# A four-layer graph network on one core: layer 3's last product in four quadrants, the last LSTM units first and alone, two small tasks later

## The chip, the cores and the metric

The kernel runs on one core of a Trainium2 chip. A core has TensorE (PE, matrix products into PSUM), VectorE (DVE), ScalarE (ACT, table functions and copies), GpSimd (POOL) and SyncE (SP, which here issues the loads and stores). Each works through its own queue of instructions in order; they meet at semaphores. The metric is the device time of one execution in microseconds.

## The reference, cut to what matters

The input x has 128 graphs of 64 nodes with 256 features, in fp32. Four layers follow each other, each as `x = layernorm(x + layer(x))`. Layer 0 is a graph convolution with two batch normalisations, layer 1 a Chebyshev step with attention and a feed-forward net, layer 2 two graph convolutions followed by LSTMs, layer 3 graph attention. The change touches layers 2 and 3:

```python
# layer 2, after two graph convolutions
for p in range(1, MAX_SKIP + 1):                     # 1, 2, 3, 4
    nw = Tv // p
    wins = h[:, :nw * p, :].reshape(Bv * nw, p, Hd)
    last = _lstm_last(Wih[p - 1], Whh[p - 1], bih[p - 1], bhh[p - 1], wins)
    idx = jnp.arange(nw) * p + (p - 1)
    h = h.at[:, idx, :].set(last.reshape(Bv, nw, Hd))
# layer 3
Wh = jnp.einsum('bnf,fo->bno', h, W)
s1 = Wh @ a1
s2 = Wh @ a2
e = s1[:, :, None] + s2[:, None, :]
e = jnp.where(e >= 0, e, ALPHA * e)
e = jnp.where(adj_matrix[None] == 0, -jnp.inf, e)
attention = jax.nn.softmax(e, axis=-1)
h_prime = jnp.einsum('bij,bjo->bio', attention, Wh)
```

An LSTM with window p walks through p nodes one after the other, and the LSTM with window p + 1 reads what the one before wrote. So for one group of graphs the four windows are a chain, and inside a window the p steps are a chain too.

## The kernel before, in words

**Tiling.** The 128 graphs are 16 blocks of 8 graphs. A block is 4 tiles of two graphs: 128 partitions (2 graphs of 64 nodes) by 256 features. Four blocks make a group of 32 graphs; layer 2's LSTMs work on groups, with features on the partitions (tile h). There are four PSUM buffers of 128x1024 (PS, named ps in the profile) and a stock of temporaries of the same size (mem, named t, and later also freed parts of x, h, wL, wA and rows).

**The plan.** Nothing is ordered by hand. Each piece of work is a Python generator (first_block, end_block, block, gcn_block, unit, last_block) that yields steps `step(engine, us, ...)`, and `flow` at build time picks, again and again, which generator goes on. It keeps a clock for each engine, and for each running generator a time at which its next step's inputs are there. The key is the line

```python
soon = max(t + margin.get(e, 0.0), free[e])
```

where t is that time, `free[e]` the time at which the engine is free, and the margin 2.0 us on TensorE and 0.5 on VectorE and ScalarE. The smallest key is emitted next; ties go to the stream with the lower priority number. So a step whose inputs are there only just now is put behind one whose inputs have been there for longer than the margin. The order made in this way is fixed in the program; on the chip each engine follows it, whatever the true durations are.

**Streams.** A stream has a width (how many of its generators run at a time) and a priority. There are two calls of `flow`: one for layer 0 up to its second normalisation, and one for all the rest. In the second, in order of priority: lending of buffers (0), `extra` (1 task each for layer 2's bias rows, gcn_rows, and layer 3's score columns, score_columns; priority 0), weight loads (1), `end` (the 8 half-blocks of layer 3 for the last group, width 4, priority 2), `gcn` (3), `seq` (layer 0's end and layer 1, width 6, priority 4), the LSTM units (5) and `last` (the 12 whole blocks of layer 3 for groups 0 to 2, width 4, priority 6).

**LSTM units.** A unit is an LSTM with window p over some windows of one group: unit(p, g, w0, nw, b0, nb). Window 1 is done in gcn_block (products at L950). Window 4 is one unit for each of groups 0 to 2, and two halves of 16 graphs, 256 columns, for group 3. Whole units use seven products in place of eight for a step (stage1 to stage4, products at L1022; gates at L1060 to L1102). The halves use plain_steps: products of the input at L1159 and of the hidden state at L1161, gates at L1164. The first step of any unit is L950 with gates at L962. The last three units of the list are (4, 2) and the two halves of (4, 3). Before the change they stand in two streams of priority 5, width 2 each: `units[:-2]` and `units[-2:]`.

**A block of layer 3.** last_block(i, t0, nt) handles nt tiles, four for a whole block and two for a half-block. It gathers h on ScalarE (L1362), transposes (L338), adds x (L1373), normalises (bn_stats L270, a power on GpSimd L306, L309 and ScalarE L312), transposes again (L332), copies to xT on ScalarE (L1384), multiplies with W and the score columns (L1397; copies L1407 and L1409), builds e (GpSimd L1417, PE L1421 and L1422, VectorE L1426 to L1430), takes exp with row sums on ScalarE (L1434), reciprocals of the sums on VectorE (L1436), transposes e in 64x64 pieces (L1442), copies them (L1444), multiplies them with Wh (L1450), scales by the reciprocal sums and adds x on VectorE (L1455), normalises and stores (L1461). The product L1450 has for each tile two 64x64 products, one for each graph, from upper partitions to upper ones and from lower to lower.

Of the kernel before, what the change touches and what calls it, by code (L numbers as in the profile page):

```python
# [11 lines left out]
ALU = mybir.AluOpType  # L12
# [3 lines left out]
P = 128  # L16
B, N, D = 128, 64, 256
# [16 lines left out]
def kernel(ctx: ExitStack, tc: tile.TileContext, a: dict, out: bass.AP):  # L34
    nc = tc.nc
    V, S, G, T = nc.vector, nc.scalar, nc.gpsimd, nc.tensor
# [5 lines left out]
    def bc_last(ap, n):  # L42

        return ap.unsqueeze(2).to_broadcast([ap.shape[0], ap.shape[1], n])

    def tm(s):

        return s.rearrange("p (t d) -> p t d", t=NT)

    def fm(s):  # L50

        return s.rearrange("p (c k) -> p c k", c=2)
# [9 lines left out]
    class Stock:  # L62


        def __init__(self, items):
            self.items, self.free, self.shut = [], [], {}
            self.add(items, 0.0)
# [30 lines left out]
    class Stream:  # L98
# [3 lines left out]

        def __init__(self, width, prio, tasks):
            self.width, self.prio, self.tasks, self.n = width, prio, tasks, 0

    done = {}

# [3 lines left out]
    def ready(*keys):  # L113

        if all(k in done for k in keys):
            return max([0.0] + [done[k] for k in keys])
        return None

    def step(e, us, ps=0, sl=0, waits=True, at=None, tbl=None):

        return (e, us, ps, sl, waits, at, tbl)

    def flow(streams, margin):
# [6 lines left out]
        free = dict.fromkeys("TVSGQ", 0.0)  # L135
        table, running, now, seq = None, [], 0.0, 0
        while True:
            for s in streams:
                while s.tasks and s.n < s.width:
                    cond, body, peak = s.tasks[0]  # L140
                    t = 0.0 if cond is None else cond()
# [27 lines left out]
            for r in running:  # L169
                e, us, ps, sl, _, at, tbl = r[2]  # L170
                at = at() if callable(at) else at
                if r[2][5] is not None and at is None:
                    continue
                t = r[3] if at is None else at
                soon = max(t + margin.get(e, 0.0), free[e])
                t = max(t, free[e])
                if (ps <= 0 or len(PS.free) >= ps) and (sl <= 0 or (len(mem.free) >= sl and safe(r, sl))):
                    if ps > 0:
                        t = max(t, PS.free[0][0])
                        soon = max(soon, PS.free[0][0])  # L180
                    if sl > 0:
                        t = max(t, heapq.nsmallest(sl, mem.free)[-1][0])
                        soon = max(soon, t)
                    if best is None or soon < least - 1e-9:
                        best, when, least = r, t, soon
            assert best is not None, "no task can go on"
            e, us, ps, sl, waits, at, tbl = best[2]
# [22 lines left out]
    def ctile(shape, name, pool=cp):  # L210
        return pool.tile(shape, F32, tag=name, name=name)
# [12 lines left out]
    PS = Stock([ctile([P, NT * D], f"ps{j}", psp) for j in range(4)])  # L224
# [16 lines left out]
    halves = slice(0, N), slice(N, P)  # L241
    for s in range(2):
        h = halves[s]
# [141 lines left out]
    with c0:  # L385
# [195 lines left out]
        tasks = [(None, lambda i=i: first_block(i), 2) for i in blocks]  # L581
# [769 lines left out]
    def last_block(i, t0=0, nt=NT):  # L1351
# [3 lines left out]
        x = tm(mem[s_x])[:, :nt, :]  # L1355
        nc.sync.dma_start(x, XD[i][:, t0 : t0 + nt, :])
        r = nt / NT
# [9 lines left out]
        ps = PS.take()  # L1367
        px = tm(PS[ps])[:, :nt, :]
# [9 lines left out]
        ps = PS.take()  # L1378
        s_xT = mem.take()
        px = fm(PS[ps])[:, :, : nt * P]  # L1380
        to_fm(px, x)
        yield step("S", 0.1 + r, ps=-1)
        xT = fm(mem[s_xT])[:, :, : nt * P]
        S.copy(xT, px)  # L1384
        PS.give(ps)
        s12 = sm.tile([P, NT, 2], F32, tag="s12", name="s12")
        for t in range(0, nt, 2):
            end = t == nt - 2
            yield step("T", 1.75, ps=1, sl=int(t == 0))
            ps = PS.take()  # L1390
            pw = fm(PS[ps])
            if t == 0:
                s_w = mem.take()
                Wh = tm(mem[s_w])
            for j in range(2):
                for k in range(2):
# [4 lines left out]
                        start=(k == 0),  # L1401
                        stop=(k == 1),
# [13 lines left out]
        e, aT, d = (mem[s_e][:, j * nt * N : (j + 1) * nt * N].rearrange("p (t m) -> p t m", t=nt) for j in range(3))  # L1416
        G.tensor_tensor(d, bc_mid(unit2, nt), bc_last(s12[:, :nt, 1], N), ALU.mult)  # L1417
        yield step("T", 0.1 + 0.9 * r, ps=1)
        ps = PS.take()
# [12 lines left out]
        sums = sm.tile([P, NT], F32, tag="sums3", name="sums3")  # L1432
        for t in range(nt):
            S.activation(e[:, t, :], e[:, t, :], AF.Exp, bias=mx[:, t : t + 1], accum_out=sums[:, t : t + 1])  # L1434
        yield step("V", 0.2, waits=False)
        V.reciprocal(sums[:, :nt], sums[:, :nt])  # L1436
        yield step("T", 0.1 + 0.5 * r, ps=1)
        ps = PS.take()
        pt = PS[ps][:, : nt * N].rearrange("p (t m) -> p t m", t=nt)
# [3 lines left out]
        yield step("S", 0.15 + 0.3 * r, ps=-1)  # L1443
        S.copy(aT, pt)  # L1444
        PS.give(ps)
        yield step("T", 0.1 + 1.8 * r, ps=1)
        ps = PS.take()
        for t in range(nt):
            for h in halves:
                T.matmul(tm(PS[ps])[h, t, :], aT[h, t, :], Wh[h, t, :], start=True, stop=True)  # L1450
        mem.give(s_e)
        mem.give(s_w)
        yield step("V", 1.7 * r, ps=-1)
        for t in range(nt):
            V.scalar_tensor_tensor(  # L1455
                x[:, t, :], tm(PS[ps])[:, t, :], sums[:, t : t + 1], x[:, t, :], ALU.mult, ALU.add
            )
        PS.give(ps)
        yield from ln_steps_act(x)
        yield step("Q", 3.0)  # L1460
# [8 lines left out]
    for i in blocks:  # L1469
        while n < at_end.get(i, NBLK):  # L1470
            j = ends[n]
# [27 lines left out]
    for g in range(NG - 1):  # L1499
        read = [("read", i) for i in range(4 * g, 4 * g + 4)]  # L1500
        again = lambda g=g: mem.add(Hs[4 * g : 4 * g + 4], Clock.end)
        lends.append(Stream(1, 0, [(lambda read=read: ready(*read), again, 0)]))
    extra = [(None, gcn_rows, 1), (None, score_columns, 1)]
    gcn = [
        (
            lambda i=i: ready(("rows",), ("l1", i), *[("h", j) for j in range(4 * (i // 4), 4 * (i // 4) + 4)])
# [34 lines left out]
    units = []  # L1541
# [12 lines left out]
    def last_of(i, *part):  # L1554
# [10 lines left out]
            Stream(4, 2, end),  # L1565
            Stream(2, 3, gcn),
            Stream(6, 4, seq),
            Stream(2, 5, units[:-2]),
            Stream(2, 5, units[-2:]),
            Stream(4, 6, last),  # L1570
        ],
        MARGIN,
# [49 lines left out]
```

## Time and profile before

| | |
|---|---|
| median of 3 runs | 2446.64 us (2445.72 to 2447.99) |
| the profiled execution | 2449.05 us; its span, first to last instruction, 2447.3 us |
| TensorE busy | 2362.6 us, 97% of the span |
| VectorE, ScalarE, GpSimd busy | 1208.8, 1152.1, 565.7 us |
| mean granted TensorE clock | 0.984 |
| L1450, the product that changes | 256 records; 12 blocks of 16, 8 half-blocks of 8 |
| L1384, the copy to xT | 0.99 us for 128x1024, 0.57 us for 128x512 |
| L1455, scaling and adding | 64 instructions of 0.476 us |
| ACT table loads at L1434 | 8, of 1.28 us each |

A profile line of the order of time has the start in us from the first instruction, the length, the engine, the line of the kernel, the operation, the tile written and the tiles read, the shapes and how many instructions were merged; in brackets the idle time of the engine before it and what ended that. PEld is TensorE's loading of weights. An fp32 product stands as two records of MATMUL.

### The profile page before, as it was taken

How to read it: one execution, taken by the hardware profiler on the slowest of the kernel's cores; microseconds unless marked ns; L12 is line 12 of the kernel's file. 1: busy time of each engine (PE TensorE's matmuls, PEld its weight loads, DVE VectorE, ACT ScalarE, POOL GpSimd, SP SyncE). 2: the span in 40 equal slices, each digit the busy share in tenths (PEclk: the TensorE clock that was granted, in tenths of full speed). 3: DMA queues.
4: the chain of work that ended last, by engine and by line, in shares of the span. 5: the costliest groups of instructions: out<-in, count | busy, mean ns of one | idle time of the engine just before them, and what ended most of it. 6: DMA issues, size and time to landing. Idle time of an engine off the chain costs nothing.

```text
span 2447.3 us, 33911 instructions
## 1 busy us (share of the span) xinstructions
PE 2362.6 (97%) x13700; PEld 1807.8 (74%) x13700; DVE 1208.8 (49%) x2868; ACT 1152.1 (47%) x2086; POOL 565.7 (23%) x426
## 2 busy tenths in 40 slices
PE   8999889989999999999999999999999999999986
PEld 5544566766775767666667888999999888888864
DVE  4542378564665455464442433354444554543465
ACT  2255454533444544444444444444435555653574
POOL 0000034231422233232322222222222222221111
PEclk9999899999999999999999999999999999999998
DMA  5110111100000000000010000000001001000201
GB/s 171 45 59 0 31 36 35 35 9 10 1 18 7 12 1 18 10 27 9 27 50 2 18 1 1 14 5 1 1 1 35 1 18 35 18 9 18 65 31 52
DMA packets 40973, 57.47 MB, mean 23 GB/s; under 512 B 4592, under 2 KB 33904, under 8 KB 40816
## 3 DMA queue, kind: packets, MB, share of 16 engines
q1 hardware_dynamic: 39712, 54.22, 6.8%
q8 instruction: 107, 1.75, 0.3%
q10 hardware_dynamic: 1104, 1.08, 0.1%
q14 instruction: 50, 0.41, 0.1%
HBM read 38.52 MB, written 16.78 MB: 23 GB/s over the span
## 4 chain that ended last, share of the span: by engine, by line
PE 73%; DVE 6%; ACT 4%; POOL 2%; issue 1%; POOLq 0%; ACTq 0%; DVEq 0%
PE ps L1022 24%; PE ps L950 13%; PE ps L344 10%; PE ps L356 5%; PE ps L833 4%; PE ps L320 3%; PE ps L703 2%; PE ps L1397 2%; PE ps L1159 2%; PE ps L1161 2%; DVE ln_st L270 1%; PE ps L332 1%; PE ps L776 1%; PE ps L1450 1%; ACT x L312 1%
## 5 line engine op out<-in xcount | busy, mean ns | idle before, releaser
L1022 PE MATMUL ps<-x,x 128*128 128x256 f32 x832 | 203.2, 379 | 0.7 <-DVE x L1090 0.7
L1022 PEld LDWEIGHTS ps<-x,x 128*128 128x128 f32 x832 | 155.0, 190 | 19.9 <-issue 1.1
L312 ACT ACTIVATE x<-x,ln_nm,ln_rs 128x256 f32<-128x256 f32 x176 | 92.9, 592 | 112.8 <-DVE ln_nm L309 112.8
L1022 PE MATMUL ps<-t,x 128*128 128x256 f32 x576 | 137.7, 380 | 0.0
L1022 PEld LDWEIGHTS ps<-t,x 128*128 128x128 f32 x576 | 108.4, 190 | 14.5 <-issue 0.4
L344 PE MATMUL ps<-t,W1T 128*128 128x512 f32 x256 | 115.1, 593 | 0.0
L306 POOL TENSOR_TENSOR ln_rs<-ln_rs,neghalf 128x4 f32<-128x4 f32 (+1 forms) x72 | 69.4, 964 | 189.7 <-DVE ln_rs L272 167.9
L950 PE MATMUL ps<-t,wL 128*128 128x512 f32 x216 | 94.5, 594 | 1.8 <-ACT t L1248 1.8
L292 POOL TENSOR_TENSOR ln_rs<-ln_rs,neghalf 128x4 f32<-128x4 f32 x32 | 35.9, 1122 | 239.5 <-DVE ln_rs L272 239.0
L950 PE MATMUL ps<-h,x 128*128 128x256 f32 x384 | 86.8, 379 | 0.0
L270 DVE BATCH_NORM_STATS2 ln_st<-x 128x6 f32<-128x256 f32 x224 | 85.5, 403 | 0.4
L962 ACT ACTIVATE t<-ps,bih 128x512 f32<-128x512 f32 (+3 forms) x108 | 63.5, 640 | 44.5 <-PE ps L950 44.4
L344 PE MATMUL ps<-t,wA 128*128 128x512 f32 x176 | 81.5, 608 | 2.6 <-ACT t L679 2.6
L1022 PE MATMUL ps<-h,x 128*128 128x256 f32 x320 | 82.5, 380 | 0.0
L1081 DVE COPY t<-ps 128x256 f32<-128x256 f32 (+2 forms) x58 | 21.6, 373 | 120.5 <-PE ps L1022 120.2
L344 PEld LDWEIGHTS ps<-t,W1T 128*128 128x128 f32 x256 | 46.3, 190 | 46.4 <-issue 46.4
L950 PEld LDWEIGHTS ps<-h,x 128*128 128x128 f32 x384 | 72.8, 190 | 10.2 <-issue 0.5
L950 PE MATMUL ps<-h,wL 128*128 128x192 f32 (+2 forms) x432 | 79.8, 338 | 0.0
L950 PEld LDWEIGHTS ps<-t,wL 128*128 128x128 f32 x216 | 40.7, 190 | 50.8 <-issue 47.1
L1098 ACT ACTIVATE x<-x,bih 128x512 f32<-128x512 f32 (+2 forms) x65 | 42.2, 650 | 76.2 <-DVE x L1088 73.9
L962 ACT ACTIVATE x<-ps,bih 128x512 f32<-128x512 f32 (+3 forms) x94 | 54.8, 636 | 45.6 <-PE ps L950 45.6
L950 PEld LDWEIGHTS ps<-h,wL 128*128 128x128 f32 x432 | 65.6, 190 | 11.4 <-issue 10.5
(681 smaller groups left out, 5765.3 us busy)
## 6 DMA issues: line engine op xcount, KB each, us to landing
t<-in_x_dram SPq DMA_DIRECT2D x28, 512.0 KB, 4.0
xd<-x SPq DMA_DIRECT2D x16, 512.0 KB, 2.6
x<-xd SPq DMA_DIRECT2D x5, 512.0 KB, 3.3
out_dram<-x SPq DMA_DIRECT2D x5, 512.0 KB, 2.9
wL<-in_L_gnn_Wih_dram SPq DMA_DIRECT2D x2, 1024.0 KB, 5.1
x<-in_L_gnn_Whh_dram SPq DMA_DIRECT2D x2, 1024.0 KB, 4.8
h<-in_x_dram SPq DMA_DIRECT2D x3, 512.0 KB, 5.0
t<-xd SPq DMA_DIRECT2D x3, 512.0 KB, 3.7
```

The lines of the kernel that those rows point to most:

```text
L270: V.bn_stats(st[:, t, :], y[:, t, :])
L306: G.tensor_tensor(rs, rs, neghalf[:, :n], ALU.pow)
L312: S.activation(y[:, t, :], y[:, t, :], AF.Identity, scale=rs[:, t : t + 1], bias=nm[:, t : t + 1])
L320: T.matmul(ps[:, c, t * P : (t + 1) * P], y[:, t, c * P : (c + 1) * P], mT, start=True, stop=True,)
L344: T.matmul(ps[:, c, :], w[:, k, (off + c) * P : (off + c + 1) * P], yT[:, k, :], start=(k == 0), stop=(k == nk - 1),)
L356: T.matmul(ps[:, t, :], yT[:, k, t * P : (t + 1) * P], w[:, k, :], start=(k == 0), stop=(k == nk - 1),)
L703: T.matmul(pv[r * N : (r + 1) * N, b, :, :], x1T[:, k, b * N : (b + 1) * N], Wv_par[:, k, r, :, :], start=(k == 0), stop=(k == 1),)
L833: T.matmul(tm(PS[ps])[:, t, :], fm(mem[gs[k // 2]])[:, k % 2, t * P : (t + 1) * P], W2[:, k, :], start=(k == 0), stop=(k == 3),)
L950: T.matmul(spread(fm(PS[ps])[:, j, :n], q), WL[p][0][:, k, m], x_of(0, q)[:, k], start=(k == 0), stop=(k == 1),)
L962: S.activation(of(sl)[:, j], fm(PS[ps])[:, j, :n], AF.Tanh if g == 2 else AF.Sigmoid, bias=bias(g, c))
L1022: T.matmul(dst, WS[p][name](k, g), y[:, k], start=first and k == 0, stop=k == 1, skip_group_check=not first)
L1159: T.matmul(shaped(dst), WL[p][0][:, k, m], x[:, k], start=(k == 0), stop=False)
```

## The change

Four edits are made together.

1. **The product L1450 in four quadrants.** For odd tiles, the two graphs change places in xT: the copy into xT becomes three copies, one of the even tiles and two of the odd tiles' halves. With that, Wh, the scores and e of odd tiles have their graphs swapped. The product of an odd tile then goes from upper partitions to lower ones and from lower to upper, which puts the graphs back, and the four products of two tiles use the four quadrants of the array, odd tiles in another PSUM bank than even ones.
2. **The softmax's scaling earlier.** e is multiplied by the reciprocal sums before its transpose, so that what follows the product is two additions and not four scaled ones. The step now counts as one that the next must wait for.
3. **The last three units.** They get a stream of their own, of width 1 (one at a time), priority 1.5, and marked urgent: for their steps `flow` leaves out the margin on every engine.
4. **The small tasks.** gcn_rows may begin only when layer 1's block 3 has begun, score_columns only after that and when layer 1's block 0 is done.

```diff
-        def __init__(self, width, prio, tasks):
+        def __init__(self, width, prio, tasks, urgent=False):
             self.width, self.prio, self.tasks, self.n = width, prio, tasks, 0
+            self.urgent = urgent
...
-                soon = max(t + margin.get(e, 0.0), free[e])
+                soon = max(t if r[6].urgent else t + margin.get(e, 0.0), free[e])
...
-        yield step("S", 0.1 + r, ps=-1)
+        yield step("S", 0.3 + 1.1 * r, ps=-1)
         xT = fm(mem[s_xT])[:, :, : nt * P]
-        S.copy(xT, px)
+        pairs, into = (ap.rearrange("p c (u e k) -> p c u e k", e=2, k=P) for ap in (px, xT))
+        S.copy(into[:, :, :, 0], pairs[:, :, :, 0])
+        for h in range(2):
+            S.copy(into[:, :, :, 1, halves[1 - h]], pairs[:, :, :, 1, halves[h]])
...
-        yield step("V", 0.2, waits=False)
+        yield step("V", 0.3 + 0.3 * r)
         V.reciprocal(sums[:, :nt], sums[:, :nt])
+        V.tensor_tensor(e, e, bc_last(sums[:, :nt], N), ALU.mult)
...
-        yield step("T", 0.1 + 1.8 * r, ps=1)
-        ps = PS.take()
-        for t in range(nt):
-            for h in halves:
-                T.matmul(tm(PS[ps])[h, t, :], aT[h, t, :], Wh[h, t, :], start=True, stop=True)
+        yield step("T", 0.1 + 0.95 * r, ps=1)
+        ps = PS.take()
+        po = PS[ps].rearrange("p (e u d) -> p e u d", e=2, u=2)
+        for t in range(0, nt, 2):
+            for j in range(2):
+                for h in range(2):
+                    T.matmul(
+                        po[halves[h ^ j], j, t // 2, :],
+                        aT[halves[h], t + j, :],
+                        Wh[halves[h], t + j, :],
+                        start=True,
+                        stop=True,
+                    )
...
-        yield step("V", 1.7 * r, ps=-1)
-        for t in range(nt):
-            V.scalar_tensor_tensor(
-                x[:, t, :], tm(PS[ps])[:, t, :], sums[:, t : t + 1], x[:, t, :], ALU.mult, ALU.add
-            )
+        yield step("V", 0.1 + 1.2 * r, ps=-1)
+        for j in range(2):
+            V.tensor_tensor(x[:, j::2, :], po[:, j, : nt // 2, :], x[:, j::2, :], ALU.add)
...
-    extra = [(None, gcn_rows, 1), (None, score_columns, 1)]
+    extra = [(lambda: ready(("begun", 3)), gcn_rows, 1), (lambda: ready(("l1", 0)), score_columns, 1)]
...
-            Stream(2, 5, units[:-2]),
-            Stream(2, 5, units[-2:]),
+            Stream(2, 5, units[:-3]),
+            Stream(1, 1.5, units[-3:], urgent=True),
             Stream(4, 6, last),
```

## The prediction

> **What bounds the kernel now.** I read the page's busy shares and slices first, then the busy time by stretch, then the order of time on TensorE and ScalarE in the last 150 us.
>
> ```profile
> PE 2362.6 (97%) x13700; PEld 1807.8 (74%) x13700; DVE 1208.8 (49%) x2868; ACT 1152.1 (47%) x2086; POOL 565.7 (23%) x426
> ...
> PE   8999889989999999999999999999999999999986
> PEclk9999899999999999999999999999999999999998
> ```
>
> TensorE is the bound nearly everywhere; it idles 2447.3 - 2362.6 = 84.7 us. The last slice is the weakest. The stretches around the last LSTM product (columns: length, then busy us and count for PE, PEld, DVE, ACT, POOL, then clock):
>
> ```profile
> 2338.90:2447.30 108.40, 80.18 (x505) 55.26 (x503) 61.28 (x255) 67.53 (x171) 20.17 (x27) 0.85 0.13 44
> 2230.00:2338.90 108.90, 108.67 (x570) 91.43 (x569) 51.09 (x150) 56.78 (x127) 18.03 (x23) 1.00 0.14 47
> ```
>
> Until that product PE is full; after it come 108.4 us in which PE sits idle for 28.2 us and has clock 0.85. That tail is layer 3's blocks alone, each one long chain. Now PE's rate for small and large products, and the start of the second plan:
>
> ```profile
> 2276.41 1.89 PE L1022 MATMUL ps<-rows,x 128*128 128x256 f32 x8
> 333.66 1.21 PE L728 MATMUL ps<-h,t 64*64 64x64 f32 x64
> 2398.57 1.94 PE L1450 MATMUL ps<-wA,x 64*64 64x256 f32 x16 [0.47 <-ACT x L1444]
> ...
> 285.66 1.94 PE L338 MATMUL ps<-ident,h 128*128 128x128 f32 x8 [2.38 <-DVE rb L888]
> 292.90 3.54 PE L903 MATMUL ps<-av,t 128*128 128x1 f32 x16 [1.95 <-DMA av<-in_L_gnn_a_dram]
> ```
>
> An fp32 product is two records. The L1022 row's 8 records take 1.73 us to the next row's start: 0.216 us per record of 256 columns. The L1450 row has 16 such records, 3.46 us in single file, and took 1.88: two at once. L728 already uses all four quadrants: 64 records of 64 columns would take 64 x 0.054 = 3.46 us in file and took 1.14 to the next start: 3.0 at once on average. The two lower rows are layer 2's small tasks, which hold PE up while it starts.
>
> **What the Trainium skill says.** "TensorEngine Tiling (Array Packing)", Tiling Modes, says that 64x64 mode has four tiles that load and multiply in parallel: the L728 row agrees. Its Restrictions and Gotchas say that different row tiles can't access one PSUM bank simultaneously: L1450's two row halves write one bank, in different partitions, and run two at once all the same, so I charge nothing for the new form, which also has two row halves in each bank. "ScalarE: Activation LUTs", What ACT_TABLE_LOAD costs, gives 1283 ns for the load and about 2.66 us with a drain; this trace has 1.28 and no visible drain:
>
> ```profile
> 2345.23 0.58 ACT L1409 COPY wL<-ps 128x512 f32<-128x512 f32 x1
> 2345.82 1.28 ACT L1434 ACT_TABLE_LOAD   x1
> 2347.11 0.35 ACT L1434 ACTIVATE wA<-wA,mx 128x64 f32<-128x64 f32 x1
> ```
>
> **The last product in four quadrants.** 12 blocks of four tiles and 8 of two are 64 tiles, 128 products, 256 records. Two at once they cost 128 x 0.216 = 27.6 us; four at once 13.8. Gain 13.8; at L728's mean of 3.0 it would be 9.2. I take 13.8, since L728's steady part is nearer to four.
>
> What pays for it: ScalarE's copy into xT (1.00 us for 128x1024, 0.57 for 128x512) becomes three, by L1409's 0.57 and L1444's 0.37 and 0.26: 0.57+2x0.37 = 1.31, or 0.37+2x0.26 = 0.89. That is +0.31 twelve times and +0.32 eight times, 6.3 us of ACT. On VectorE a multiply of 128x256 (0.41, as L1426) is added and two adds of 128x512 (0.67, as L1373) replace four of 0.476: 0.41+1.34-1.90 = -0.15 per block, nothing. The wait: the transposes L1442 now stand behind reciprocal and multiply, some 0.7 us (0.17+0.41+two hops of 0.1) later in each block's chain; behind them on PE stand other streams' products. Other blocks cover it, except in the last block, which gets 0.5 back from the shorter product.
>
> **The small tasks later.** L338 started at 285.66 behind the copies L887/L888, while its input was scaled by 284.4 (two of ACT's twelve L636 of 0.71 from 282.95): up to 1.3 us. L903 held PE for 3.5 us at a low clock, but the aggregation behind it waited for L312, which ended at 296.2, 0.2 before it. In the new order another block's add (L644, 1.23) goes in between the first block's normalisation steps. I take -1, from -4 to +2. Their loads leave SP's queue, where it waited 10.4 us at L375 and 4.7 at L896 for a free buffer with the input blocks' loads behind them; those now come first, and the tasks' own stand later, before anything needs them (their results feed layer 2's and layer 3's blocks, which begin after layer 1's).
>
> **The last three units.** I counted PE work by the order of the two programs, at 0.43 us per 256-column product and in proportion. Before, 68.5 us of full-clock PE work follow the last LSTM product; 108.4 - 68.5 = 39.9 us of the tail are idle time and low clock. After, the twelve whole blocks stand earlier, among the steps of the two halves of (4,3), and only 18.6 us follow. What is left is four half-blocks. ACT per half-block: gather copies 2x0.65, two normalisations 4x0.55, xT 0.89, Wh 0.57, exp with its sums 2x0.52, aT 0.26: 6.3 us, four times 25. Ahead: gates, cell and h, about 2.9 (0.81+2x0.42+0.40+2x0.43); behind: the store, 3.5 (issued 2443.8, end 2447.3). If ACT never waits: 31.4. One half-block alone, summed over its rows with 25 hops of 0.1, is about 27.6; with no overlap on ACT 27.6+3x6.3 = 46.4. I take the middle, 38. So 38-18.6 = 19.4 replace 39.9: -20.5 (-27 to -12).
>
> The price of being first with no margin: a step is now placed where its input should just be there; before, PE steps had 2.0 us to spare. PE is in order, so every late step stops everything behind it. In the new order the recurrent products of the two halves of (4,3) come 2.5 to 6 us of PE work after the last product of the step before, and the chain between (gates 0.84, two VectorE steps, tanh, one more) is 2.2 at the first step and about 3.1 later: mostly covered. But the planner counts 0.3 us per tile for the exponentials and the trace shows 0.52, so a whole block's exp ends 0.9 late, and the table changes between exp and sigmoid 31 times in the last phase against 15: 16x1.28 = 20.5 us more of ACT. ACT is 52% busy in the second stretch above, so this is hidden as busy time; without that cover it would cost 26.8 with the copies. About 11 whole blocks fall beside urgent units; if a third of their 0.9 shows, 3.3, and 84 dependent urgent steps (60 in (4,2), 24 in the halves) at 0.04 give 3.4. I take +6.5, from 0 to +35.
>
> **Sum.** -13.8 -1 -20.5 +6.5 = -28.8 against the profiled span: 2447.3 to 2418.5. That execution took 2449.05 in all, 2.4 above the median of 2446.64; taking the difference off the median gives 2418.
>
> **Rivals.** (1) *The stalls move*: TensorE waits at urgent steps for about as long as the tail gives back, some 15 us more than I allow: 2433. For it: in-order engines, 31 table loads. Against: the distances above. (2) *Slower*: exposed urgent steps become the bound. Without stalls the gain is 35.3; 84 steps at over 0.42 us each eat it. Price at 0.6 us: 50, so 2461. For it: even with the margin, PE shows waits of 0.5 to 1.4 us at L1022 around 2025 to 2095. Against: these were few, and the planner's numbers for LSTM steps agree with the rows (0.69 for an add that takes 0.69). (3) *The quadrants run only in pairs*: -15, so 2433; against it speaks L728. (4) *More*: the whole second plan is reordered, since the greedy planner differs from the first moved task on; some 50 us of PE idle outside the tail, 20 of them before 400 us, could shrink too: 2400. It could as well grow by as much, which is in the range.
>
> **Chances.** Forecast 0.55 (own range 2408 to 2428), (1) 0.16, (2) 0.11, (3) 0.06, (4) 0.12. Two in ten are left outside 2402 to 2437. A difference of 0.2% (4.9 us) is what a measurement can tell from none: faster 0.84, within it 0.05 from the edges of (1) and (3), slower 0.11.
>
> **What would show it.** L1450's row for four tiles takes about 1.0 us instead of 1.9, and PE's busy sum falls by about 14. After the last L1161 there remain 34 to 46 us. PE's idle time in the 150 us before that product stays under 10 us, and waits there name ACT's gates (L1164) or DVE's adds. Table loads on ACT rise by about 16. Wrong if L1450's group keeps 1.9 us; if waits at the urgent L1022 and L1161 sum to over 20 us; or if idle time between 400 and 2200 us changes by over 10 us either way, which would be the reordering and no part of my sum.

## The result and the profile after

The changed kernel takes 2439.8 us (median of 10 runs, 2435.6 to 2441.3) against 2447.1 us for the kernel before (10 runs beside it). The ratio is 0.9968, with a 95% interval from 0.9960 to 0.9976: 7.4 us, or 0.32%, faster. The direction was predicted; the size was not. 2418 was forecast, and the measured time lies just above 2437, the upper end of the range.

The profiled execution took 2439.17 us with a span of 2437.4 us, 9.9 us less than the span before. In the changed kernel the lines have moved: L1022 is L1024, L1161 is L1163, the copies to xT are L1389 and L1391, the exponentials L1441, the transposes of e L1450, the product L1460, the last additions L1471. First the busy times and the slices of the page:

```profile
PE 2348.3 (96%) x13700; PEld 1798.9 (74%) x13700; DVE 1215.1 (50%) x2864; ACT 1169.9 (48%) x2138; POOL 566.7 (23%) x426
...
PE   8999889999999999999999999999999999998997
```

TensorE's busy sum has fallen by 14.3 us, and the share by a point: with a shorter span, idle time has grown from 84.7 to 89.1 us. Of the last four slices, 9, 9, 8, 6 before, the first is now 8, and the last two are 9 and 7: the tail is denser, and a gap has opened ahead of it. Next the busy time by stretch (length, then busy us and count for PE, PEld, DVE, ACT, POOL, then the clock, the DMA share and GB/s), for the part after the last LSTM product and for 160 us shortly before it:

```profile
2398.70:2437.40 38.70, 22.70 (x161) 16.35 (x160) 22.48 (x101) 26.67 (x71) 8.48 (x14) 0.74 0.14 48
...
2180.00:2340.00 160.00, 146.53 (x950) 120.60 (x949) 87.01 (x290) 127.60 (x287) 29.98 (x34) 0.98 0.16 53
```

The tail is 38.7 us where it was 108.2, and PE idles in it for 16.0 us where it was 28.2. But in the stretch ahead of it PE now idles for 13.5 of 160 us, at a clock of 0.98, while ScalarE is busy for 80% of the time. In the kernel before, a stretch of the same length that also ends some 59 us ahead of the last LSTM product looked like this:

```profile
2120.00:2280.00 160.00, 159.97 (x849) 139.71 (x848) 65.54 (x154) 76.56 (x182) 28.21 (x27) 1.00 0.04 14
```

And the product, in the order of time of the kernel after:

```profile
2054.70 1.67 PE L1024 MATMUL ps<-x,x 128*128 128x256 f32 x7
2056.31 1.09 PE L1460 MATMUL ps<-t,x 64*64 64x256 f32 x16
2057.33 0.92 PE L1024 MATMUL ps<-x,x 128*128 128x256 f32 x3
```

Sixteen records now take 1.02 us to the next row's start, where they took 1.88: 16 x 0.216 / 1.02 = 3.4 at once with the fill and drain in it. Over the whole program the line's busy time falls from 36.3 to 18.6 us; that is more than 13.8, since before some of these rows ran at half clock in the tail.

**Where the 9.9 us of the span come from.** TensorE's time falls into three parts, by the first L1024 of the windows above 1 and by the last LSTM product:

| | before | after |
|---|---|---|
| PE busy | 2362.6 | 2348.3 |
| PE idle up to the first L1022 / L1024 (1309.0; 1299.7 us) | 46.3 | 52.3 |
| PE idle from there to the last LSTM product | 10.3 | 20.8 |
| PE idle in the tail | 28.2 | 16.0 |
| length of the tail | 108.2 | 38.7 |
| table loads, all / after the first L1022 | 61 / 15 | 73 / 31 |

The sum is -14.3 + 6.0 + 10.5 - 12.2 = -10.0, the whole difference but for rounding. Two terms gave back 16.5 us. The first of these is older than it looks. Between 1650 and 1920 us both programs issue the same products in the same order, so one row of each can be held against the other. Before, and then after:

```profile
1871.75 1.13 PE L1022 MATMUL ps<-x,x 128*128 128x256 f32 x4 [0.66 <-DVE x L1090]
```

```profile
1881.38 1.13 PE L1024 MATMUL ps<-x,x 128*128 128x256 f32 x4 [0.66 <-DVE t L1092]
```

At that point the changed kernel, none of whose new products and urgent units has run yet, is 9.6 us *behind*. Four other waits between 1653 and 1917 us give 9.6 to 9.7 as well. From there to the end it gains 19.5 us. Only the fourth edit, the later start of the two small tasks, changes the order of the program that early.

The experiments below say how firm this is. Ten of them have TensorE's products up to this row in the order of the kernel before; they and that kernel reach it at 1869.5 to 1873.2 us. The fourth edit alone reaches it at 1882.1. Of the 9.6 us, 6.2 are idle time (47.6 before, 53.8 after; 45.2 to 48.1 in the eleven with the old order). The other 3.4 are busy time, 1824.2 and 1827.6 us, and come only in part from the order. Up to this row TensorE's clock stood at half for 47.8 us before and for 54.6 after; four of the ten with the old order have 54.6 us, too, and are busy for 1825.6 to 1826.7.

### The profile page after: what moved, and what is told of

Same layout as the page of the kernel before. It is cut to its first block, busy times and chain, and to the rows that moved or that the text cites. A ratio compares the mean times of both kernels' runs of the same rounds, so it can differ in the third digit from the quotient of the medians.

```text
span 2437.4 us, 33965 instructions
## 1 busy us (share of the span) xinstructions
PE 2348.3 (96%) x13700; PEld 1798.9 (74%) x13700; DVE 1215.1 (50%) x2864; ACT 1169.9 (48%) x2138; POOL 566.7 (23%) x426
## 5 line engine op out<-in xcount | busy, mean ns | idle before, releaser
L1024 PE MATMUL ps<-x,x 128*128 128x256 f32 x1024 | 248.6, 380 | 0.7 <-DVE t L1092 0.7
L1024 PEld LDWEIGHTS ps<-x,x 128*128 128x128 f32 x1024 | 191.5, 190 | 26.4 <-issue 1.6
L1024 PE MATMUL ps<-t,x 128*128 128x256 f32 x576 | 141.0, 379 | 0.0
L1024 PEld LDWEIGHTS ps<-t,x 128*128 128x128 f32 x576 | 108.6, 190 | 14.6 <-issue 0.4
L952 PE MATMUL ps<-h,wL 128*128 128x192 f32 (+2 forms) x504 | 111.6, 375 | 0.0
L952 PEld LDWEIGHTS ps<-h,wL 128*128 128x128 f32 x504 | 79.1, 190 | 27.6 <-issue 26.7
L1100 ACT ACTIVATE t<-t,bih 128x512 f32<-128x512 f32 (+2 forms) x63 | 41.0, 652 | 107.6 <-DVE t L1090 105.9
L952 PE MATMUL ps<-h,x 128*128 128x256 f32 x384 | 86.8, 379 | 0.0
L346 PEld LDWEIGHTS ps<-t,W1T 128*128 128x128 f32 x256 | 46.3, 190 | 46.4 <-issue 46.4
L952 PEld LDWEIGHTS ps<-h,x 128*128 128x128 f32 x384 | 72.9, 190 | 10.3 <-issue 0.5
L1083 DVE COPY t<-ps 128x256 f32<-128x256 f32 (+2 forms) x63 | 23.7, 378 | 113.5 <-PE ps L1024 113.5
L273 DVE BATCH_NORM_AGGREGATE ln_mv<-ln_st 128x2 f32<-128x6 f32 x448 | 71.3, 167 | 0.0
L346 PE MATMUL ps<-t,wA 128*128 128x512 f32 x144 | 67.9, 617 | 2.8 <-ACT t L681 2.8
L952 PE MATMUL ps<-t,wL 128*128 128x512 f32 x144 | 64.9, 607 | 2.5 <-ACT t L1250 2.5
L1090 DVE TENSOR_TENSOR t<-ps,t 128x512 f32<-128x512 f32 (+2 forms) x63 | 38.1, 604 | 54.8 <-PE ps L1024 47.9
```

Of the source, the lines that this page charges most:

```text
L273: V.bn_aggr(mv[:, t, :], st[:, t, :])
L346: T.matmul(ps[:, c, :], w[:, k, (off + c) * P : (off + c + 1) * P], yT[:, k, :], start=(k == 0), stop=(k == nk - 1),)
L952: T.matmul(spread(fm(PS[ps])[:, j, :n], q), WL[p][0][:, k, m], x_of(0, q)[:, k], start=(k == 0), stop=(k == 1),)
L1024: T.matmul(dst, WS[p][name](k, g), y[:, k], start=first and k == 0, stop=k == 1, skip_group_check=not first)
L1090: V.tensor_tensor(y[:, 0:2, :], v[:, 2:4, :], y[:, 0:2, :], ALU.add)
L1100: S.activation(of(act[g])[:, 0], of(act[g])[:, 0], f, bias=bias(g, 0))
```

## The experiments

All ratios are to the kernel before on the same chip, with 95% intervals. Two theories stood at the start. *Reorder*: moving the small tasks makes the planner order layer 1 anew, and this order is some 10 us worse; the other edits are worth more than the result shows. *Stalls*: the urgent units wait for ScalarE, and this eats the gain; the small tasks are innocent.

### One edit out, and one edit alone

The change without its fourth edit:

```diff
-    extra = [(lambda: ready(("begun", 3)), gcn_rows, 1), (lambda: ready(("l1", 0)), score_columns, 1)]
+    extra = [(None, gcn_rows, 1), (None, score_columns, 1)]
```

> The changed kernel with the two small tasks at their old place; the quadrants and the urgent stream stay. Theory A (moving the small tasks reordered layer 1 and cost the 9.6 us by which the changed kernel is behind at 1300 us): 2430, some 10 us faster than the changed kernel, with TensorE's idle time between 500 and 1300 us back from 19.8 to about 13. Theory B (the small tasks are worth the -1 of the prediction, and the missing time went to steps placed without a margin): about 2441, no faster than the changed kernel.

Measured: 2427.9 us, 0.9923 (0.9909 to 0.9936). The fourth edit costs the change about 12 us. The kernel before with this edit alone:

```diff
-    extra = [(None, gcn_rows, 1), (None, score_columns, 1)]
+    extra = [(lambda: ready(("begun", 3)), gcn_rows, 1), (lambda: ready(("l1", 0)), score_columns, 1)]
```

> The kernel before with the small tasks moved and nothing else. Theory A: slower than before by 8 to 11 us, about 2456, with all of it lost by 1300 us. Theory B: 2446, equal within the noise.

Measured: 2460.2 us, 1.0055 (1.0042 to 1.0067), 14 us slower than the kernel before. In busy time by stretch, from 500 to 1300 us, of the kernel before, the change, the change without the edit, and the edit alone, in this order:

```profile
500.00:1300.00 800.00, 786.74 (x5121) 542.78 (x5120) 427.07 (x965) 351.09 (x446) 241.46 (x148) 0.99 0.04 15
```

```profile
500.00:1300.00 800.00, 780.17 (x5087) 540.24 (x5086) 433.19 (x949) 341.95 (x436) 239.01 (x145) 0.99 0.04 15
```

```profile
500.00:1300.00 800.00, 786.72 (x5121) 541.98 (x5120) 428.41 (x970) 349.90 (x445) 241.74 (x148) 0.99 0.04 15
```

```profile
500.00:1300.00 800.00, 780.15 (x5088) 540.34 (x5087) 433.75 (x950) 341.92 (x436) 239.05 (x145) 0.99 0.04 15
```

The two kernels with the edit leave PE idle for 19.8 us, the two without it for 13.3, whatever else they have. So the reorder theory holds for this part of the loss.

Edits 1 and 2, the product and the scaling, on the kernel before:

```diff
-            Stream(2, 5, units[:-3]),
-            Stream(1, 1.5, units[-3:], urgent=True),
+            Stream(2, 5, units[:-2]),
+            Stream(2, 5, units[-2:]),
```

> The kernel before with the product in four quadrants and the earlier scaling, the old streams and the old place of the small tasks. Both theories: TensorE busy about 14 us less; 2433 if all of it reaches the end, down to 2430 where the part of the product that ran at a low clock in the tail counts more, 2440 if half of it turns into idle time in the tail's chains.

(The diff is against the change without its fourth edit.) Measured: 2437.9 us, 0.9963 (0.9950 to 0.9975): 8.3 us of the 13.8 reach the end (6 to 12 by the interval). PE is busy for 2342.8 us, and its idle time between the first L1022 and the last LSTM product grows from 10.3 to 17.4 us, although no unit is urgent here. The tail in it, by stretch:

```profile
2357.70:2433.80 76.10, 48.95 (x376) 36.34 (x374) 43.64 (x187) 50.10 (x144) 15.88 (x22) 0.86 0.15 49
```

27.2 us of PE idle time in the tail, almost as many as before (28.2), at a clock of 0.86, before 0.85. So the shorter product takes no idle time out of the tail, and the 7.1 us that were added to it ahead of the tail take part of the gain back. What adds them was not tested; the three copies and the later transposes are candidates, and the plan has 19 table loads there in place of 15.

Edit 3, the urgent units, on the kernel before:

```diff
...
-                soon = max(t + margin.get(e, 0.0), free[e])
+                soon = max(t if r[6].urgent else t + margin.get(e, 0.0), free[e])
...
-            Stream(2, 5, units[:-2]),
-            Stream(2, 5, units[-2:]),
+            Stream(2, 5, units[:-3]),
+            Stream(1, 1.5, units[-3:], urgent=True),
```

> The kernel before with the last three units in the urgent stream and nothing else. The tail after the last LSTM product should fall from 108 to about 40 us in both theories. Theory A: waits of last_block steps behind ScalarE's table loads eat about 12 of the 20 us that the tail gives: 2439, with ScalarE over 75% busy in the stretch of the two last halves. Theory B: waits at steps without margin eat all of it or more: 2447 to 2455, and the waits stand at the products of the urgent units (L1022, L1159, L1161).

Measured: 2439.8 us (10 runs), 0.9977 (0.9968 to 0.9986), a gain of 6.4 us. The tail is 47.1 us, and idle time in the last phase 15.3. Alone, the two pieces give 8.3 + 6.4 = 14.7; together, without the small tasks' edit, they give 18.3. Whether they help each other isn't shown: the 3.6 us between these sums are within the intervals.

### Is it the tasks' place or the order?

If being late were what costs, the later the task the more it should cost. Three other placements test that. The bias rows late and the score columns straight after them, with nothing else to wait for:

```diff
-    extra = [(lambda: ready(("begun", 3)), gcn_rows, 1), (lambda: ready(("l1", 0)), score_columns, 1)]
+    extra = [(lambda: ready(("begun", 3)), gcn_rows, 1), (None, score_columns, 1)]
```

> The changed kernel with the bias rows after the beginning of layer 1's block 3, as in the change, and the score columns straight after them instead of after block 0's end. If the loss of the change's fourth part belongs to the late bias rows: 2438 to 2442, as in the changed kernel, with TensorE busy about 780 us between 500 and 1300 us. If it belongs to this one order that the planner happened to make: another value, on either side, from 2422 to 2445, with busy time between 500 and 1300 us near 786.

Measured: 2427.8 us, 0.9921 (0.9904 to 0.9937). Only the score columns late, behind layer 1's block 0:

```diff
-    extra = [(lambda: ready(("begun", 3)), gcn_rows, 1), (lambda: ready(("l1", 0)), score_columns, 1)]
+    extra = [(None, gcn_rows, 1), (lambda: ready(("l1", 0)), score_columns, 1)]
```

> The changed kernel with only one of the small tasks moved: the bias rows at their old place at the start, the score columns after layer 1's block 0. If the loss of 10 to 14 us belongs to the bias rows, which the second layer's blocks wait for: 2428, as with both tasks early. If it belongs to the score columns: 2440, as in the changed kernel. If any new order of layer 1 brings its own idle time, by the greedy planner's choice and not by one task: a third value between 2420 and 2445.

Measured: 2430.0 us, 0.9927 (0.9912 to 0.9942). And the change with the rows one block later still:

```diff
-    extra = [(lambda: ready(("begun", 3)), gcn_rows, 1), (lambda: ready(("l1", 0)), score_columns, 1)]
+    extra = [(lambda: ready(("begun", 4)), gcn_rows, 1), (lambda: ready(("l1", 0)), score_columns, 1)]
```

> The changed kernel with the bias rows after the beginning of layer 1's block 4 instead of block 3, the score columns as in the change. If late bias rows cost by themselves, the cost is the same or larger: 2440 or more. If the loss is the planner's accident: no relation to the delay, anything from 2422 to 2445.

Measured: 2453.1 us, 1.0022 (1.0012 to 1.0032), 13 us slower than the change. By stretch, the rows-late kernel and then this one:

```profile
280.00:500.00 220.00, 200.46 (x1534) 147.18 (x1535) 149.07 (x414) 118.77 (x171) 75.07 (x53) 0.95 0.13 41
500.00:1300.00 800.00, 787.81 (x5132) 542.61 (x5130) 420.31 (x941) 349.28 (x443) 240.04 (x145) 1.00 0.04 15
```

```profile
280.00:500.00 220.00, 191.74 (x1507) 146.29 (x1508) 157.11 (x435) 110.81 (x159) 74.97 (x53) 0.93 0.13 43
500.00:1300.00 800.00, 778.83 (x5064) 533.39 (x5063) 426.85 (x893) 352.79 (x447) 240.28 (x143) 0.99 0.03 13
```

The traces tell where the tasks came to stand. The bias rows' copies (L889) start at 285 us where the task is early, at 367 in the change, at 369 in the rows-late kernel and at 477 a block later; the products of the score columns (L905) start at 293, 424 and 378 us, at 437 with only these late, and at 484 in the last kernel. So the rows cost nothing as late as in the change, if the score columns follow them directly (2427.8 against 2427.9), and the score columns cost little still later than in the change, if the rows are early (2430.0). The two placements together cost 12 us, and a block later 25. Taken alone, the last two experiments would have spoken for the rival, that late bias rows cost by themselves: 2430.0 with the rows early, 2453.1 with them later still, which is also outside the 2422 to 2445 that I had given to an accident of the order. The rows-late kernel speaks against it. A cost of the pair, both late and apart, isn't excluded.

The orders differ in idle time: from 500 to 1300 us it is 12 to 21 us, and a block later adds 28.3 us in the 220 us before, where the rows-late kernel has 19.5. So it is the greedy order of layer 1 that each placement leads to, as far as is known; which single step of it is bad stays open. PE's longest waits from 500 to 1300 us are three of 3.4 to 3.5 us in the change and one of 5.8 us in the kernel before, at different lines, and in the 6 us of added idle time no one wait stands out.

### What costs the 10 us in the last phase?

The change without the fourth edit (2427.9) still idles for 20.1 us between the first L1024 and the last LSTM product, against 10.3 before. Three suspects: the table loads between exp and the gates; the urgent units' missing margin; the planner's price of 0.3 us per tile for exponentials that take 0.52. All experiments of this part but the one on the kernel before are edits of that kernel. One caution goes for all that follows: only the replacement of the sigmoid leaves the plan's order as it is. Every other edit makes the planner choose anew, and orders alone were seen to differ by 12 to 25 us.

Table loads. The gates of windows above 1 take, at all three places, tanh in place of sigmoid, which leaves the sigmoid out of the computation but keeps every instruction's size and the plan; exp, tanh and gates then need no loads between them:

```diff
...
-                f = AF.Tanh if g == 2 else AF.Sigmoid
+                f = AF.Tanh if g == 2 or p > 1 else AF.Sigmoid
...
```

> The changed kernel with the small tasks at their old place, and with tanh in place of sigmoid in the LSTM units of windows 2 to 4, so that ScalarE needs no change of table between the units' gates and layer 3's exponentials. The sigmoid of these units is left out of the computation. Theory A1 (the waits between the first L1022 product and the last LSTM product, 20 us in this version and 10 in the kernel before, come from ScalarE, which is over 80% busy around 2250 us with 31 table loads): those 20 fall to 12 or less, time 2417 to 2421. Theory A2 (they come from steps placed without a margin, whatever ScalarE does): they stay at 18 or more, time 2425 to 2429.

Measured: 2414.9 us, 0.9866 (0.9852 to 0.9881), 13 us less; loads in the last phase fall from 31 to 1, idle time in it from 20.1 to 10.6 us. By stretch, the kernel without the fourth edit and then this one:

```profile
2180.00:2340.00 160.00, 146.03 (x929) 119.64 (x929) 87.87 (x299) 128.26 (x292) 32.14 (x38) 0.98 0.14 45
```

```profile
2180.00:2340.00 160.00, 155.99 (x997) 129.35 (x996) 87.80 (x309) 109.55 (x289) 35.07 (x42) 1.00 0.16 54
```

ScalarE is busy for 109.6 us in place of 128.3, PE for 156.0 in place of 146.0, and its clock is 1.00 again. In the whole last phase the waits that ScalarE ended fall from 9.0 to 5.3 us, and those that VectorE ended from 9.8 to 5.2. The mechanism can be read off one place. On ScalarE, in the change as it is:

```profile
2186.48 1.28 ACT L1441 ACT_TABLE_LOAD   x1
2187.77 0.35 ACT L1441 ACTIVATE t<-t,mx 128x64 f32<-128x64 f32 x1
...
2189.02 0.19 ACT L1441 ACTIVATION_READ_ACCUMULATOR t<-t,mx 128x1 f32 x1
2189.22 1.28 ACT L1100 ACT_TABLE_LOAD   x1
2190.52 0.53 ACT L1100 ACTIVATE t<-t,bih 128x288 f32<-128x288 f32 x1
...
2191.26 0.36 ACT L1104 ACTIVATE t<-ps,bih 128x144 f32<-128x144 f32 x1
```

and on TensorE at the same time:

```profile
2188.40 0.76 PE L1024 MATMUL ps<-h,wA 128*128 128x144 f32 x4 [0.16 <-DVE x L1092]
2191.68 0.88 PE L1450 MATMUL ps<-ident,t 64*64 64x64 f32 x16 [2.52 <-ACT t L1104]
```

One block's exponentials, 1.45 us of work, come between two loads, 4.0 us in all, and the gates of the unit that was to be first on every engine stand behind them. PE's next product is held until L1104 has ended. The two share no data; most likely the product takes the PSUM buffer that this gate reads and so gives back. The same place without loads, ScalarE and then TensorE:

```profile
2174.96 0.19 ACT L1441 ACTIVATION_READ_ACCUMULATOR t<-t,mx 128x1 f32 x1
2175.05 0.52 ACT L1100 ACTIVATE t<-t,bih 128x288 f32<-128x288 f32 x1
...
2176.25 0.38 ACT L1104 ACTIVATE t<-ps,bih 128x144 f32<-128x144 f32 x1
```

```profile
2175.77 0.76 PE L1024 MATMUL ps<-h,wA 128*128 128x144 f32 x4 [0.16 <-DVE x L1092]
2176.68 0.68 PE L1450 MATMUL ps<-ident,t 64*64 64x64 f32 x16 [0.16 <-ACT t L1104]
```

2.52 us of waiting have become 0.16; the two loads were 2.56.

Is this a cost of the change, or did the kernel before have it too? The same replacement there, with the sigmoid again left out of windows above 1:

> The kernel before with tanh in place of sigmoid in the LSTM units of windows 2 to 4, so that 14 of its 15 table loads of the last phase go. The sigmoid of these units is left out of the computation. If table loads cost because the urgent units stand among layer 3's exponentials (the change's own 16 more loads): little here, 0 to 3 us less than before, since the margin of 2 us hides them. If each load costs the same 0.43 us anywhere: 6 us less. If tanh in place of sigmoid is itself faster on ScalarE: 10 us or more less.

Measured: 2445.0 us, 0.9992 (0.9983 to 1.0001), a gain of 2.2 us that can hardly be told from none. It also excludes that tanh is itself so much faster than sigmoid. So some 11 of the 13 us, a difference of two measured gains, belong to the change.

The margin. The last three units keep their stream but lose the urgent mark, so that their steps have 2.0 us to spare on PE again:

```diff
-            Stream(1, 1.5, units[-3:], urgent=True),
+            Stream(1, 1.5, units[-3:]),
```

> The changed kernel with the small tasks at their old place; the last three units keep their own stream, one at a time and at priority 1.5, but the planner's margins hold for them again. Theory A1: the table loads stay (75 in the program against 77), so the idle time before the last LSTM product stays within 4 us of 20 and the time within 4 us of 2428. Theory A2: idle time before the last LSTM product falls to about 12 and the time to 2420, unless the last product comes later because the units are begun later.

Measured: 2436.2 us, 0.9956 (0.9939 to 0.9973), 8 us slower than with the mark, and the idle time in the last phase is 23.7 us. Neither expectation had that time. Keeping the margin gains nothing here; since the order is another one, this doesn't price the margin alone.

The planner's price:

```diff
-        yield step("S", 0.3 * nt, tbl="exp")
+        yield step("S", 0.52 * nt, tbl="exp")
```

> The changed kernel with the small tasks at their old place, and the planner's price of layer 3's exponentials raised from 0.3 to 0.52 us per tile, which is what the profile shows. Theory A3 (the plan is late by 0.9 us at each whole block since it prices the exponentials too low): idle time before the last LSTM product falls by 3 to 6 us, 2422 to 2425. If the price is not what matters: within 2 us of 2428, or a few us worse by another order.

Measured: 2433.9 us, 0.9943 (0.9928 to 0.9958); idle time 20.5 us, the tail 43.7 where it was 38.5. Telling the planner the true duration gains nothing, so nothing shows the price as the cause.

### Can the whole computation have those 13 us?

With the sigmoid's table alone: exp(z) is s/(1-s) with s the sigmoid of z, so the softmax needs no other table, at the price of four VectorE instructions per block (a step's price and the name of its table change with it, and are left out here):

```diff
-            S.activation(e[:, t, :], e[:, t, :], AF.Exp, bias=mx[:, t : t + 1], accum_out=sums[:, t : t + 1])
+            S.activation(e[:, t, :], e[:, t, :], AF.Sigmoid, bias=mx[:, t : t + 1])
...
+        V.tensor_scalar(d, e, -1.0, 1.0, ALU.mult, ALU.add)
+        V.reciprocal(d, d)
+        V.tensor_tensor(e, e, d, ALU.mult)
+        V.reduce_sum(sums[:, :nt], e, axis=AX.X)
```

> The changed kernel with the small tasks at their old place, and layer 3's exponentials taken as s / (1 - s) with s the sigmoid, so that they need the table that the LSTM gates use; VectorE forms 1 - s, the reciprocal, the product and the row sums. The computation is whole. Theory A1 (table loads hold ScalarE up and TensorE behind it): 2414 to 2420, the 31 table loads of the last phase gone and the idle time before the last LSTM product near 11. Rival: VectorE's four further operations, about 1.5 us in each block's chain and some 27 us in all, take the place of the table loads: 2424 to 2429.

Measured: 2434.0 us, 0.9946 (0.9932 to 0.9961). There is no load left in the last phase, but PE still idles for 19.7 us there, and the tail has grown to 52.2 us. VectorE, in the order of time:

```profile
2393.28 0.29 DVE L1443 TENSOR_SCALAR t<-t 128x256 f32<-128x256 f32 x1
...
2394.37 1.74 DVE L1444 RECIPROCAL t<-t 128x256 f32<-128x256 f32 x1
...
2396.37 0.41 DVE L1445 TENSOR_TENSOR t<-t 128x256 f32<-128x256 f32 x1
...
2397.36 0.41 DVE L1446 TENSOR_REDUCE sums<-t 128x4 f32<-128x256 f32 x1
```

The reciprocal takes 1.74 us, more than a load, and stands in every whole block's chain and in VectorE's queue. Of the idle time in the last phase VectorE ended 11.9 us and ScalarE 7.7, where the kernel without loads has 5.2 and 5.3. So VectorE has most likely taken ScalarE's place; what the new order adds to it wasn't separated, and the time is above both expectations.

With fewer loads: the planner puts off each step that would change between exp and another table by 6 or by 10 us, so that several blocks' exponentials come together:

```diff
+                if "exp3" in (tbl, table) and tbl not in (None, table):
+                    soon += 10.0
...
-        yield step("S", 0.3 * nt, tbl="exp")
+        yield step("S", 0.3 * nt, tbl="exp3")
```

> The same with 6 us instead of 10: 67 table loads, 21 of them in the last phase. By the number of loads: 4.3 us less than with 31, 2423.5. If only the order's accidents matter: no relation to the number, 2420 to 2434.

> The changed kernel with the small tasks at their old place, the whole computation, and a planner that from the first exponential of layer 3 on puts a step that needs another table 10 us further back in its choice. The program then has 57 table loads instead of 77, 11 of them in the last phase instead of 31. If the number of loads is what cost 13 us (0.43 us each, from 30 loads taken away): 8.7 us less, 2419, with the idle time before the last LSTM product near 14. If the kernel without loads won by its changed values or by a luckier order: 2426 to 2432.

Measured: 21 loads in the last phase and 2463.8 us, 1.0072 (1.0057 to 1.0087), with 6 us; 11 loads and 2470.9 us, 1.0099 (1.0082 to 1.0116), with 10 us, far above anything expected. By stretch, the kernel with 10 us:

```profile
2300.00:2400.00 100.00, 65.13 (x504) 47.11 (x504) 64.15 (x248) 67.98 (x183) 19.58 (x23) 0.78 0.27 90
```

A third of the time PE has nothing to do, at a clock of 0.78. "ScalarE: Activation LUTs" in the Trainium skill, in its section on table sets, advises to batch calls by set. Here the loads fell by two thirds and the kernel became 43 us slower than without the batching. In the stretch above only 16 of PE's 504 records belong to LSTM units and 488 to blocks; in the kernel without batching, 264 of 544 belong to units in the 100 us that end as far before its last LSTM product. So the batching has pulled the blocks together, away from the LSTM products that covered them, and PE waits for the blocks' own chains: its two longest waits, of 7.2 and 6.3 us, name their normalisation on ScalarE. How much of the 43 us is this, and how much an accident of the order, isn't separated. How to get the 13 us with the whole computation stays open.

## Why the prediction was off

**The product: right.** L1460's row for four tiles takes 1.09 us, as "about 1.0 instead of 1.9" said, and I had chosen the upper of my two rates. At full clock a row of 16 records saves 0.86 us and one of 8 some 0.42, over 12 and 8 of them 13.7. That PE's busy sum falls by 14.3 is partly a coincidence, since low clock is in that sum, too: the line itself fell by 17.7, and other lines rose. What I had not said is that on its own the edit brings only 8.3 us to the end, with 7.1 us more idle time in the last phase.

**The tail: right in its mechanism, and in part by luck in its size.** 38.7 us remain where I took the middle of 31.4 and 46.4 for 38 (it is 38.9). The two ends were worked out; that the middle is so near was not. With 18.6 us of full-clock work in it, 20.1 of idle time and low clock replace 39.7 (108.2 - 68.5), a gain of 19.6 against the 20.5 of the sum.

**The small tasks: the step that failed.** "I take -1, from -4 to +2" priced two rows at the start, L338 and L903, and the places next to them in the queues. (Of these only L903 belongs to a small task, layer 3's score columns; L338 is a transpose that stood behind the bias rows' copies.) The term put at nothing that from the first moved task on the planner orders layer 1 differently. It measured +9.6 us in the span and +12 to +14 in the times. I did name the reordering, but as rival (4), where I gave it 0.12 with a *gain*, with the remark that it could as well grow; it belonged in the sum with a spread of both signs. The sign I set for it went unobserved: idle time between 400 and 2200 us changed by 3.8 us (from 24.0 to 27.8), not by 10. It rose by about 6 up to the first L1024 and fell by about 2 after it, and the rest of the shift was no idle time. (The idle time named with that rival was read too low at the start: outside the tail it was 56.5 us, 32.3 of them before 400.) Holding identical rows of the two programs against each other, as above, shows the shift at once.

**The price of being first: mechanism right, size too small by half.** The term of +6.5 came out as some 14 us: what is left of the -9.9 when -13.8, -19.6 and +9.6 are taken out; 10.5 of it is idle time. This is a remainder and no measurement of the urgent units alone: the quadrants without them already add 7.1 us of idle time in the last phase, and the urgent units without the quadrants 5.0. The 20.5 us of table loads had been put at nothing because ScalarE was 52% busy. That was the share of the stretch *before* the change; in the stretch that the change makes, with blocks and urgent gates together, it is 80%, and a load isn't spread over idle time but stands directly ahead of a gate that PE waits for. The cover was gone, and I had its price, 26.8 us with the copies; about half showed, and some 11 of the 14, by the replacement of the sigmoid, go with the loads. The two reasons that I gave for the 6.5, exponentials priced too low and dependent steps without a margin, found no support: the experiments on each gave no gain. Table loads rose by 16, as I had said, but the other signs hardly moved. Waits at L1022 and L1161 (now L1024 and L1163) sum to 7.7 us in the last phase, before 7.1, since the wait falls on whatever product stands next in PE's queue. PE's idle time in the 150 us before the last LSTM product is 7.1 us, under the 10 that I had allowed (before 0.2), and 13.7 us stand ahead of those 150. From 2180 to 2400 us, in the list of waits (total us, times, longest):

```profile
PE ps L1450 <- ACT t L1104: 2.5, 1, 2.5
PE ps L1163 <- DVE h L1193: 1.9, 1, 1.9
PE ps L1404 <- DVE ln_st L272: 1.8, 1, 1.8
PE ps L334 <- ACT h L1104: 1.7, 1, 1.7
```

Of the four longest, two are a block's products held by a gate.

**The rivals.** (1), stalls that move, has the nearest number, 2433, and about half of its 15 us are there, by another cause than I gave. (2), slower, didn't come. (3), pairs only, is excluded by L1460's row (its sum would have given 2432, not 2433). (4) named the cause of the failed step, with the wrong sign. Without the small tasks' edit the kernel takes 2427.9: the sum without that step would have been some 9 us too low, and inside its range.

## What to carry to other kernels

Where a greedy planner fixes the order at build time, a task that is moved is not priced by its own rows: try a few neighbouring placements of it, since here five of them differ by 25 us with no rule found behind it, and leaving it where it was (2427.9) beats the changed kernel by 12 us and the one before by 18. Work that is taken out of a tail and put beside other work has to be costed with the busy shares of the stretch that results; a table load ahead of a gate in ScalarE's queue can be a wait of its full length for whoever needs that gate (2.52 us here behind two loads of 1.28, 0.16 without them). And before batching such loads, check what the batch starves.

## What the runs showed of the hardware that was not expected

- VectorE's RECIPROCAL of 128x256 fp32 takes 1.74 us and of 128x128 0.95, so about 6.2 ns per further column, where a TENSOR_TENSOR of 128x256 takes 0.41 in all. "VectorE: DVE Perf Modes" in the Trainium skill (First, the fixed hardware budget) says that reciprocal is an iterative divide with a repeat count of 8; no run here shows the repeats, only the duration.
- Four 64x64 products in four quadrants, two row halves in each PSUM bank, run at 3.4 at once over 16 records with fill and drain, and no slowing from a shared bank shows.
- In the 16 traces of this case PE's granted clock has two values only, 1.0 and 0.5, and every figure between them is a mean over time. Low clock comes with idle time (0.98 with 14 us idle in 160, 1.00 with 4, 0.78 with 35 in 100), but the idle share alone doesn't fix it: the tail of the kernel before, 26% idle, has 0.85, and that of the quadrants alone, 36% idle, has 0.86. And it varies between executions: where the eleven kernels with the old order reach one and the same row, those with 44.4 us at half clock were busy for 1822.4 to 1823.1 us, those with 54.6 for 1825.6 to 1826.7, with the same products and about the same idle time.
